# A new order of work in the two state-space mixers of a ten-stage kernel

## The chip, the cores and the metric

One Trainium2 chip, one core of it. The time is device microseconds from the start of the program to its end. The kernel runs on five engines that follow their own instruction queues and meet at semaphores: PE (matrix products into the eight PSUM banks), DVE (vector), ACT (scalar functions from tables), POOL (a second vector engine) and SP, whose queue here only issues DMA transfers. Every array of the calculation is float32.

## The reference, cut to what matters

`x` has two rows (sequences) of 512 tokens and 256 features. Four layers follow one another, each as half a feed-forward block, a mixer, half a feed-forward block. The change lies in the mixers of layers 2 and 3 and in the feed-forward block ahead of layer 2's mixer:

```python
x = x + 0.5 * _L2_ffn_ref(_layernorm(x), ...)     # top 1 of 8 dense experts
x = x + _L2_attn_ref(_layernorm(x), ...)          # mixer, 8 heads of 64
x = x + 0.5 * _L2_ffn_ref(_layernorm(x), ...)
x = x + 0.5 * _L3_ffn_ref(_layernorm(x), ...)     # top 2 of 8 gated experts and a shared one
x = x + _L3_attn_ref(_layernorm(x), ...)          # mixer, 64 heads of 64
x = x + 0.5 * _L3_ffn_ref(_layernorm(x), ...)
```

Both mixers compute the same thing, in layer 3 with eight times as many heads:

```python
zxbcdt = u @ W_in                     # z, x|B|C and one dt for each head
dt = softplus(dt + dt_bias)
xBC = silu(conv4(xBC) + conv_b)       # 4 taps along the tokens
A = -exp(A_log)                       # decay of a token: exp(A * dt)
Y_diag = einsum('bcln,bcsn,bhcls,bcshp->bclhp', Cm, Bm, Lmat, x * dt)
states = einsum('bcln,bhcl,bclhp->bchpn', Bm, decay_states, x * dt)
Y_off  = einsum('bcln,bchpn,bhcl->bclhp', Cm, states_so_far, out_decay)
y = Y_diag + Y_off + x * D_param
yf = y * silu(z)
out = (yf * rsqrt(mean(yf * yf) + 1e-5) * norm_w) @ W_out
```

Within a chunk of tokens every token takes from the earlier ones, weighed by `Lmat` (`Y_diag`); between chunks a state of 128 by 64 for each head is carried on (`Y_off`).

## The kernel before, in words

**Tiles and steps.** `mamba` (L2079) serves both mixers. It cuts the tokens of a row into CB=4 chunks of 128. A unit is one row and one group of 8 heads, that is 512 inner columns in NM=4 pieces `m` of 128; a step is one chunk of one unit. Layer 2 has 2 units and 8 steps (`few` is true), layer 3 has 16 units and 64 steps. What is needed before the first step is the head (L2487 to L2575); the loop over the steps is L2589 to L2643.

**What sets the order.** The program's own order is written by hand. Inside `with self.in_order(tail)` (L230) each instruction of an engine is tied behind the one written before it on the same engine: in the head for PE, ACT and DVE, in the steps for POOL too. So each engine is a queue in the order of the calls, and an instruction that waits holds up all behind it on its engine. DMAs go out on SP's queue in the order written.

**The head.** `row(0)` makes the normalized, turned input `xT`; layer 2's comes already turned from the feed-forward block before (`next_measure` and `next_turn`, L1908 to L1920, into `nxT`). `decay_sums` (L2122) is a generator of which `next(d0)` runs one part: PE's product `pd` for `dt`, the softplus on ACT (`Exp`, then `Ln`), `dA`, row sums that go out to HBM as `rows` (L2171) and come back broadcast over all partitions, the sums `jb`, and last the exponentials `cd` (decay of a whole chunk) and `dec` (decay to a chunk's end), each a small PE product and an `Exp` (L2181). `conv` (L2188) is one convolution of 128 channels over a row: PE writes `pp`, ACT makes the first tap (L2196), DVE adds three taps (L2200), ACT does the SiLU (L2204). `conv_b` and `conv_c` do it for B and C; `prep_front` (L2273) for a piece of x, as `xc`, and `prep_back` (L2287) turns `xc` on PE, copies it on ACT as `xt` (L2291) and multiplies `xc` by D, for three pieces of the first unit on POOL (L2295), otherwise on ACT (L2297). `products` (L2217) are C times B of each chunk and `mask` (L2228) writes their lower triangle into the PSUM tile `M`, DVE into an SBUF tile `Msb` and ACT from there.

**The parts of a step `s`.** `chunk(s+3)` fetches the row sums by DMA into `lm` (L2308) and `ce` (L2311). `exponents` (L2316) are eight DVE operations on `lm`; `raised` (L2325) is ACT's `exp` of `lm` and `ce` together, 2048 columns, or `raised_alone` (L2328) of 1024; `masked` (L2331) is DVE's `lm` times `M`; `from_start` (L2337) is POOL's `ce` times C; `to_end` (L2358) is POOL's `xd`, x by `dec`. `z_gate` (L2343) is PE's product `pz` and ACT's SiLU of it, `sg`. `main` (L2366) is PE's `py` from `lm`, `xt`, `ce` and the state, and POOL's state by `cd` (L2385). `gate` (L2399) adds D's part on DVE and multiplies by `sg` on POOL; `squares` (L2405) and `all_squares` (L2418) sum y's squares, `project` (L2430) multiplies by `W_out` into `yacc`, `new_state` (L2387) makes `pst` on PE and adds it to the state. `add_row` (L2442) closes a row: the sum over channels `pr` (L2446), a root, and the add into `x` (L2451).

**The loop before**, the same for both layers: squares(s-1); chunk(s+3); at an odd chunk exponents(s+2), at an even one masked(s); the next unit's convolution and its taps; the turn of the piece before; z_gate(s+1); to_end(s); the SiLU of the new piece; raised(s+1) at an odd chunk, masked(s+1) at an even one; from_start(s+1); main(s); gate(s); at an even chunk exponents(s+2); all_squares and project(s-1); at the start of a row add_row of the row before; new_state(s). In layer 2's first two steps B's and C's convolution of the second row follow (`convs`). `prep_front` and `z_gate(0)` stand so that main(s) is written behind the convolution, the turn and the gate of the unit to come.

**Layer 3's expert rows.** The feed-forward block before leaves its experts' outputs in HBM. They are added to `x` by pending parts that `settle` (L261) runs: a DMA `y<-rows` (L857) and adds of 128x256 (L880), here on POOL. Row 1, the second one, is settled at the end of the head.

**PSUM.** In layer 2's feed-forward block one pool of eight banks, `psM`, serves the logits `pl`, the turned weights `ps_ct`, the experts' products `ps_y` and all turns.

## Time and profile before

| | us |
|---|---|
| median of 9 runs | 1840.26 |
| lowest and highest | 1836.88, 1846.09 |
| the profiled execution | 1833.76 |
| its span on the core | 1832.0 |
| layer 2's mixer in the trace, head and steps | 828 to 936 |
| layer 3's mixer, head | 1120 to about 1167 |
| layer 3's mixer, steps | to about 1720 |

The page of the profile gives each engine's busy time over the span, the same in 40 slices, the DMA queues, the chain of waits that ended last and the costliest groups of instructions. Three groups that belong to the mixers, each with its count, the busy time, the mean of one and the idle time just before it with what ended most of it:

```profile
L2200 DVE SCALAR_TENSOR_TENSOR xc<-pp,L_attn_cols,xc 128x511 f32<-128x511 f32 (+2 forms) x216 | 161.3, 748 | 25.3 <-ACT xc L2196 20.1
L2348 PE MATMUL pz<-lateT,wt 128*128 128x128 f32 x1024 | 125.8, 276 | 6.3 <-ACT xt L2291 4.1
L2433 PE MATMUL yacc<-wt,y 128*128 128x256 f32 x576 | 142.7, 391 | 0.6 <-DVE x L2451 0.3
```

Names come from the program: `xc<-pp` writes the tile `xc` from the tile `pp`. The line numbers are those of the kernel before. A view by windows gives the same busy times for stretches of the span, so that stages with different limits can be told apart, and a view in order of time gives start, length, engine, line and operation of each run of equal instructions, with the wait ahead of it in brackets.

### The profile page before, as it was taken

The page shows a single profiled execution, that of the slowest core. Times are in us where ns is not written, and L with a number is a line of the kernel's source. Part 1 is how long each engine was busy: PE and PEld are TensorE (multiplying, and loading weights), DVE is VectorE, ACT ScalarE, POOL GpSimd, SP SyncE. Part 2 cuts the span into 40 slices and gives each one's busy share as a digit, 9 for nine tenths or more (in the row PEclk, how much of TensorE's full clock was granted, in tenths as well). Part 3 has the DMA queues.
Part 4 walks back from the last instruction along what each step waited for, and adds up shares of the span by engine and source line. Part 5 has one row for each costly group of instructions (what it writes and reads, how often), then busy time and mean ns, then how long its engine had stood idle before and what let it go on. Part 6 is the DMA issues. An engine that isn't in the chain of part 4 may idle for free. (4 is left out here: it accounts for less than half of the span.)

```text
span 1832.0 us, 29511 instructions
## 1 busy us (share of the span) xinstructions
PE 1697.1 (93%) x10342; PEld 1220.7 (67%) x10342; DVE 1137.1 (62%) x2945; ACT 810.0 (44%) x1399; POOL 952.2 (52%) x974
## 2 busy tenths in 40 slices
PE   7999989999999889998889898799999999999994
PEld 4777756666777657545655476577777777777573
DVE  6433367346433479775867534887777887778633
ACT  1223235331223137315631123678877777777221
POOL 4777656514777441211440263546756656767373
PEclk9999999999999899999989999999999999999897
DMA  9466451142655510102300133444445444443133
GB/s 298 140 221 188 150 189 38 60 138 77 184 186 171 200 59 2 47 1 82 113 28 12 38 107 114 164 147 159 156 139 175 158 146 167 158 159 129 37 115 97
DMA packets 122197, 226.52 MB, mean 124 GB/s; under 512 B 22398, under 2 KB 74988, under 8 KB 121894
## 3 DMA queue, kind: packets, MB, share of 16 engines
q1 hardware_dynamic: 97046, 179.08, 29.5%
q0 software_dynamic: 18944, 42.16, 7.3%
q10 hardware_dynamic: 6032, 3.10, 0.6%
q8 instruction: 91, 1.49, 0.3%
q14 instruction: 84, 0.69, 0.1%
HBM read 195.59 MB, written 41.81 MB: 130 GB/s over the span
## 5 line engine op out<-in xcount | busy, mean ns | idle before, releaser
L645 POOL DMA_INDIRECT xe<-table,sl_get x176 | 183.0, 1040 | 145.1 <-DVE sl_get L617 88.1
L673 PE MATMUL ps_gu<-we,xeT 128*128 128x352 f32 x704 | 225.1, 460 | 0.0
L704 POOL DMA_INDIRECT rows<-ye,sl_put x176 | 177.1, 1006 | 88.3 <-issue 40.2
L2200 DVE SCALAR_TENSOR_TENSOR xc<-pp,L_attn_cols,xc 128x511 f32<-128x511 f32 (+2 forms) x216 | 161.3, 748 | 25.3 <-ACT xc L2196 20.1
L698 PE MATMUL ps_ye<-we,hT 88*128 88x256 f32 x704 | 168.2, 379 | 3.7 <-DVE hT L225 2.0
L678 DVE SCALAR_TENSOR_TENSOR he<-se,xe,ps_gu 128x176 f32<-128x176 f32 x176 | 69.9, 397 | 158.5 <-ACT se L677 150.5
L673 PEld LDWEIGHTS ps_gu<-we,xeT 128*128 128x128 f32 x704 | 126.1, 190 | 55.3 <-DVE xeT L225 1.4
L698 PEld LDWEIGHTS ps_ye<-we,hT 88*128 88x128 f32 x704 | 133.1, 190 | 37.9 <-ACT ye L227 3.6
L2321 DVE SCALAR_TENSOR_TENSOR lm<-lm,jb,top 128x128 f32<-128x128 f32 x576 | 153.5, 342 | 0.0
L2403 POOL TENSOR_TENSOR y<-y,sg 128x512 f32<-128x512 f32 x72 | 91.8, 1275 | 101.1 <-DVE y L2402 99.7
L2433 PE MATMUL yacc<-wt,y 128*128 128x256 f32 x576 | 142.7, 391 | 0.6 <-DVE x L2451 0.3
L677 ACT ACTIVATE se<-ps_gu 128x176 f32<-128x176 f32 x176 | 55.9, 318 | 183.8 <-PE ps_gu L673 183.8
L2348 PE MATMUL pz<-lateT,wt 128*128 128x128 f32 x1024 | 125.8, 276 | 6.3 <-ACT xt L2291 4.1
L2341 POOL TENSOR_TENSOR ce<-ce,CT 128x1024 f32<-128x1024 f32 x54 | 128.0, 2370 | 0.0
L2348 PEld LDWEIGHTS pz<-lateT,wt 128*128 128x128 f32 x1024 | 119.7, 192 | 9.5 <-ACT xt L2291 5.3
L1964 PE MATMUL ps_y<-w8T,xT 128*128 128x512 f32 x256 | 125.5, 620 | 0.0
L2193 PE MATMUL pp<-lateT,wx 128*128 128x512 f32 x256 | 121.8, 599 | 0.8 <-DVE xc L2200 0.8
L2433 PEld LDWEIGHTS yacc<-wt,y 128*128 128x128 f32 x576 | 103.8, 190 | 22.8 <-issue 9.3
L2414 POOL TENSOR_TENSOR sqs<-sqs,sq 128x512 f32<-128x512 f32 x56 | 71.3, 1274 | 85.4 <-ACT sq L2413 85.4
L2333 DVE TENSOR_TENSOR lm<-lm,M 128x1024 f32<-128x1024 f32 x72 | 87.2, 1215 | 39.3 <-ACT lm L2326 36.8
L2376 PE MATMUL py<-lm,xt 128*64 128x128 f32 x1152 | 107.1, 279 | 4.7 <-PE pz L2348 2.1
L2193 PEld LDWEIGHTS pp<-lateT,wx 128*128 128x128 f32 x256 | 48.6, 191 | 57.2 <-issue 52.3
(520 smaller groups left out, 3501.9 us busy)
## 6 DMA issues: line engine op xcount, KB each, us to landing
lm<-rows SPq DMA_DIRECT2D x72, 512.0 KB
ce<-rows SPq DMA_DIRECT2D x54, 512.0 KB
y<-rows SPq DMA_DIRECT2D x16, 768.0 KB
we<-in_L_ffn_w_gate_dram SPq DMA_DIRECT2D x64, 176.0 KB
we<-in_L_ffn_w_up_dram SPq DMA_DIRECT2D x64, 176.0 KB
we<-in_L_ffn_w_down_dram SPq DMA_DIRECT2D x64, 176.0 KB
we<-in_L_ffn_w_dram SPq DMA_DIRECT2D x48, 176.0 KB
wx<-in_L_attn_in_proj_w_dram SPq DMA_DIRECT2D x16, 512.0 KB
```

What stands on the lines that cost most here:

```text
L645: nc.gpsimd.indirect_dma_start(xe[:, i, :], None, table, bass.IndirectOffsetOnAxis(get[:, at + j : at + j + 1], 0), bounds_check=T - 1, oo ...
L673: nc.tensor.matmul(pg, xeT[:, k, i * P : (i + 1) * P], wgu[:, :, k], start=(k == 0), stop=(k == KD - 1))
L698: nc.tensor.matmul(py[:, i, :], hT[:, q, i * P : (i + 1) * P], wd[:, q, :], start=(q == 0), stop=(q == 1))
L704: put_rows = nc.gpsimd.indirect_dma_start(rows, bass.IndirectOffsetOnAxis(put[:, at + j : at + j + 1], 0), y[:, i, :], None, bounds_check= ...
L1964: nc.tensor.matmul(ps, xT[:, k, :], self.w8T[:, k, 2 * e2 : 2 * e2 + 2, :], start=(k == 0), stop=(k == KD - 1))
L2193: nc.tensor.matmul(pp, wv[:, k, :], xT[:, k, b * S : (b + 1) * S], start=(k == 0), stop=(k == KD - 1))
L2200: nc.vector.scalar_tensor_tensor(out[:, 3 - w :], pp[:, : S - 3 + w], cw[:, m, w : w + 1], out[:, 3 - w :], ALU.mult, ALU.add)
L2321: nc.vector.scalar_tensor_tensor(k["lm"][:, h, :], k["lm"][:, h, :], jb[:, k["c"], n : n + 1], top, ALU.add, ALU.min)
L2341: nc.gpsimd.tensor_tensor(k["ce"], k["ce"], ct, ALU.mult)
L2348: nc.tensor.matmul(pz[:, m, :], u["wz"][:, kk, m * P : (m + 1) * P], xT[:, kk, c * P : (c + 1) * P], start=(kk == 0), stop=(kk == KD - 1),)
L2376: nc.tensor.matmul(py[i * HP : (i + 1) * HP, m, :], w[:, h * HP : (h + 1) * HP], v[:, h, :], start=(m == 0 and n == 0), stop=(n == len(src ...
L2433: nc.tensor.matmul(yacc[cc // 2][:, cc % 2, :], k["y"][:, m, :], u["wo"][:, m, :], start=(u["g"] == 0 and m == 0 and cc % 2 == 0), stop=(u ...
```

## The change

**The feed-forward block ahead of layer 2's mixer** (`l2_ffn`). The logits and the turned weights get a PSUM pool of their own, `psG` with two banks (tags `pl` and `ct`), the rest keeps six. The last of the eight chunks is no longer normalized and turned for the mixer within the block: its scale is computed at the block's end, and the mixer calls `self.last()`, which centres it, and turns it in `decay_sums`, behind the first seven chunks of `pd`.

**Both mixers.** `cd` and `dec` share one tile and one `Exp`, so `decay_sums` has one part fewer. The first row's products are written into `M` itself and masked there. All four products of `xc` and D of the first unit are on POOL. `z_gate(0)` leaves the head and is issued in step 0; `masked(0)` enters the head, behind exponents(1).

**Layer 2.** The head has another order. The sum of squares over the four pieces is two adds on POOL in place of a reduction on DVE. The steps are issued by a function of their own, `short_step`, in which main(s), gate(s) and new_state(s) come ahead of the next convolution, turn, gate and the exponents and mask of the steps to come.

**Layer 3.** `settle(1)`, the DMAs and POOL's adds for the second row, moves from the end of the head to before `conv_c`; C's taps come ahead of the chunks' DMAs, the products ahead of the first SiLU of x. The steps are as before, apart from `z_gate(0)` and `masked(0)`.

The core of the diff, with eight columns of indent taken off:

```diff
@@ -1863,6 +1863,7 @@
+    self.lastn = keep.tile([P, D], F32, name="lastn")
@@ -1892,7 +1893,8 @@
-    psM = es.enter_context(tc.tile_pool(name="f2m", bufs=8, space=PSUM))
+    psG = es.enter_context(tc.tile_pool(name="f2g", bufs=1, space=PSUM))
+    psM = es.enter_context(tc.tile_pool(name="f2m", bufs=6, space=PSUM))
@@ -2025,8 +2027,9 @@
-        next_measure(NC - 1)
-        next_turn(NC - 1)
+        if into is not None:
+            mv, rstd = self.scale(self.keep, "n_last", NC - 1)
+            self.last = lambda: self.centre(self.lastn, NC - 1, mv, rstd)
@@ -2112,8 +2115,8 @@
-    dec = sb.tile([P, NC, nh], F32, name="dec")
-    cd = sb.tile([P, NC, nh], F32, name="cd")
+    falls = sb.tile([P, 2, NC, nh], F32, name="falls")
+    cd, dec = falls[:, 0], falls[:, 1]
@@ -2126,9 +2129,11 @@
-        pd = psM.tile(sh, F32, tag="mm", name="pd")
+        pd = (psA if few else psM).tile(sh, F32, tag="py" if few else "mm", name="pd")
         for cc in range(nb * CB):
             c = b * CB + cc
+            if few and c == NC - 1:
+                turn_last()
@@ -2178,12 +2183,17 @@
-        for out, lhsT in ((cd, self.ones), (dec, self.c["gt"])):
-            ps = aux.tile(sh, F32, tag=tag, name="ps_dec")
-            nc.tensor.matmul(ps, lhsT, da, start=True, stop=True)
-            nc.scalar.activation(out[:, bs, :], ps, AF.Exp)
-            yield
+        ps = aux.tile([P, 2] + sh[1:], F32, tag=tag, name="ps_dec")
+        for i, lhsT in enumerate((self.ones, self.c["gt"])):
+            nc.tensor.matmul(ps[:, i], lhsT, da, start=True, stop=True)
+        nc.scalar.activation(falls[:, :, bs, :], ps, AF.Exp)
+        yield
         nc.vector.tensor_tensor(dec[:, bs, :], dec[:, bs, :], d, ALU.mult)
+
+    def turn_last():
+        for k in range(KD):
+            nc.tensor.transpose(M[:, k, :], self.lastn[:, k * P : (k + 1) * P], self.ident)
+        nc.scalar.copy(xT[:, :, T - P :], M[:, :KD, :])
@@ -2226,11 +2236,12 @@
-        m = wk.tile([P, CB, P], F32, tag="xd", name="Msb")
+        m = M if pm is M else wk.tile([P, CB, P], F32, tag="xd", name="Msb")
         nc.vector.tensor_tensor(
             m, pm, self.c["le"][:, :P].unsqueeze(1).to_broadcast([P, CB, P]), ALU.mult
         )
-        nc.scalar.copy(M, m)
+        if pm is not M:
+            nc.scalar.copy(M, m)
@@ -2291,7 +2302,7 @@
-        if u["b"] == u["g"] == 0 and m < NM - 1:
+        if u["b"] == u["g"] == 0:
             nc.gpsimd.tensor_scalar(u["xc"][:, m, :], u["xc"][:, m, :], dcol[:, n : n + 1], None, ALU.mult)
@@ -2421,9 +2432,14 @@
+            if few:
+                half = sqs[:, cc, : 2 * P]
+                nc.gpsimd.tensor_tensor(half, half, sqs[:, cc, 2 * P :], ALU.add)
+                nc.gpsimd.tensor_tensor(sqm[0][:, cc, :], half[:, :P], half[:, P:], ALU.add)
+            else:
+                nc.vector.tensor_reduce(
+                    sqm[0][:, cc, :], sqs[:, cc, :].rearrange("p (m t) -> p t m", m=NM), AX.X, ALU.add
+                )
@@ -2494,14 +2510,15 @@
         if few:
             b_taps, b_silu = conv_b(0)
             c_taps, c_silu = conv_c(0)
+            self.last()
+            unit(0)
             b_taps()
+            x = [prep_front(us[0], 0)]
             c_taps()
+            x[0][0]()
             next(d0)
-            unit(0)
...
             next(d0)
             b_taps()
             unit(0)
+            self.settle(1, adder=nc.gpsimd)
             c_taps, c_silu = conv_c(0)
             next(d0)
             x = [prep_front(us[0], 0), prep_front(us[0], 1)]
             next(d0)
+            c_taps()
@@ -2512,65 +2529,60 @@
-        if not few:
+        if few:
+            x.append(prep_front(us[0], 2))
+            b_silu()
+            c_silu()
+            fill(4)
+            pm = products(0)
+            x[0][1]()
+            x[2][0]()
+            next(d0)
+            x.append(prep_front(us[0], 3))
+            x[1][1]()
+        else:
...
-            c_taps()
...
+            pm = products(0)
...
+        mask(pm)
+        prep_back(us[0], 0)
+        if not few:
             x[2][0]()
-        else:
-            x.append(prep_front(us[0], 2))
-            b_silu()
-            c_silu()
-            x[0][1]()
-            fill(4)
-            x[2][0]()
-            next(d0)
-            x.append(prep_front(us[0], 3))
-            x[1][1]()
-        pm = products(0)
...
-        if few:
-            x[3][0]()
-            mask(pm)
-        else:
-            mask(pm)
-            x[3][0]()
+        x[3][0]()
         prep_back(us[0], 1)
         x[3][1]()
         prep_back(us[0], 2)
-        z_gate(ks[0])
...
         next(d0)
-        next(d0)
         exponents(ks[1])
+        masked(ks[0])
         raised_alone(ks[1])
         next(d0, None)
-        if few:
-            later = {}
-        else:
-            self.settle(1, adder=nc.gpsimd)
+        if not few:
             parts = [lambda: measure(1), None, lambda: norm(1), lambda: turn(1, 0), lambda: turn(1, 1)]
-            parts += [d1.__next__] * 8 + [lambda: next(d1, None)]
+            parts += [d1.__next__] * 7 + [lambda: next(d1, None)]
@@ -2585,8 +2597,69 @@
-    convs = ((0, 0), (0, 1)) if few else ((NG - 4, CB - 1), (NG - 3, CB - 1))
+    convs = (NG - 4, CB - 1), (NG - 3, CB - 1)
+    def short_step(s):
+        n, cc = steps[s]
+        nxt, row_end = n + 1 < len(order), cc == CB - 1
+        k, ahead = ks[s], s + 2 < NS
+        nonlocal back
+        with self.in_order(tail):
+            if s > 0:
+                squares(ks[s - 1])
+            chunk(s + 3)
+            if back and cc == 0:
+                prep_back(*back)
+                back = None
+            if cc == 0 and s > 0:
+                masked(k)
+            rest = None
+            if s == 0:
+                taps, rest = prep_front(unit(n + 1), cc)
+                z_gate(k)
+            to_end(k)
+            main(k)
+            gate(k)
+            if s + 1 < NS:
+                from_start(ks[s + 1])
+            if s > 0:
+                all_squares(ks[s - 1])
+            new_state(k)
+            if cc % 2 and ahead:
+                exponents(ks[s + 2])
+                raised(ks[s + 1])
+            if nxt:
+                if s > 0:
+                    taps, rest = prep_front(unit(n + 1), cc)
+                taps()
+            if back:
+                prep_back(*back)
+                back = None
+            if s + 1 < NS:
+                z_gate(ks[s + 1])
+            if rest:
+                rest()
+                back = (us[n + 1], cc)
+            if s > 0:
+                project(ks.pop(s - 1))
+            if (n, cc) == (0, 0):
+                both(conv_b(1))
+            elif (n, cc) == (0, 1):
+                both(conv_c(1))
+            if cc % 2 == 0:
+                if ahead:
+                    exponents(ks[s + 2])
+                masked(ks[s + 1])
+            elif not row_end:
+                masked(ks[s + 1])
+            if n and cc == 0:
+                add_row(n - 1)
+            if nxt and row_end:
+                mask(products(1))
...
     for s in range(NS):
+        if few:
+            short_step(s)
+            continue
@@ -2601,7 +2674,7 @@
-            elif cc % 2 == 0:
+            elif cc % 2 == 0 and s > 0:
@@ -2610,6 +2683,8 @@
+            if s == 0:
+                z_gate(k)
```

More of the change, by code (lines that the diff above doesn't have):

```diff
@@ L1939, in gates @@
                     return
-                pl = psM.tile([P, E], F32, tag="mm", name="pl")
+                pl = psG.tile([P, E], F32, tag="pl", name="pl")
                 for k in range(KD):
@@ L1973, in bias_turn @@
                     return
-                ct = psM.tile([E, P], F32, tag="mm", name="ps_ct")
+                ct = psG.tile([E, P], F32, tag="ct", name="ps_ct")
                 nc.tensor.transpose(ct, ws[c], self.ident)
@@ L2218, in products @@
                 pb = psM.tile([P, CB, P], F32, tag="mm", name="pb")
-                pm = psM.tile([P, CB, P], F32, tag="mm", name="pm")
+                pm = psM.tile([P, CB, P], F32, tag="mm", name="pm") if b else M
                 for cc in range(CB):
@@ L2423, in all_squares @@
                         sqm[0] = wk.tile([P, CB, P], F32, tag="cr", name="sqm", bufs=1)
-                    nc.vector.tensor_reduce(
-                        sqm[0][:, cc, :], sqs[:, cc, :].rearrange("p (m t) -> p t m", m=NM), AX.X, ALU.add
-                    )
+                    if few:
[6 more added lines that the diff above has]
+                        )
             yacc = [psA.tile([P, 2, D], F32, name=f"yacc{i}") for i in range(CB // 2)]
@@ L2496, in mamba @@
                     c_taps, c_silu = conv_c(0)
+                    self.last()
+                    unit(0)
                     b_taps()
+                    x = [prep_front(us[0], 0)]
                     c_taps()
+                    x[0][0]()
                     next(d0)
-                    unit(0)
-                    x = [prep_front(us[0], 0)]
+                    x.append(prep_front(us[0], 1))
                     next(d0)
-                    x[0][0]()
-                    x.append(prep_front(us[0], 1))
                     next(d0)
@@ L2535, in mamba @@
                     x[1][1]()
+                mask(pm)
+                prep_back(us[0], 0)
+                if not few:
                     x[2][0]()
-                else:
-                    x.append(prep_front(us[0], 2))
-                    b_silu()
-                    c_silu()
-                    x[0][1]()
-                    fill(4)
-                    x[2][0]()
-                    next(d0)
-                    x.append(prep_front(us[0], 3))
-                    x[1][1]()
-                pm = products(0)
-                prep_back(us[0], 0)
-                x[2][1]()
-                if few:
-                    x[3][0]()
-                    mask(pm)
-                else:
-                    mask(pm)
-                    x[3][0]()
+                x[2][1]()
+                x[3][0]()
                 prep_back(us[0], 1)
```

## The prediction

> **What bounds the kernel now.** I read the page first, then busy time by stage, then the order of time inside the two stages that the diff touches.

> ```profile
> span 1832.0 us, 29511 instructions
> PE 1697.1 (93%) x10342; PEld 1220.7 (67%) x10342; DVE 1137.1 (62%) x2945; ACT 810.0 (44%) x1399; POOL 952.2 (52%) x974
> ...
> PE 4%; issue 1%; DMA 1%; POOL 0%; DVE 0%; ACT 0%; SPq 0%; POOLq 0%; ACTq 0%
> ```

> PE is the bound as a mean. The chain of waits breaks off after some 6% of the span, so it says nothing of the mixers; the stages must be read by windows (columns: stretch, length, busy time and count of PE, PEld, DVE, ACT, POOL, then granted clock, DMA share, GB/s):

> ```profile
> 828.00:870.00 42.00, 33.55 (x163) 22.25 (x161) 25.21 (x57) 23.87 (x38) 8.81 (x7) 0.92 0.26 90
> 870.00:935.00 65.00, 59.18 (x458) 45.71 (x458) 50.74 (x98) 41.82 (x56) 30.85 (x22) 1.00 0.26 91
> ...
> 1120.00:1160.00 40.00, 34.55 (x152) 23.35 (x151) 28.89 (x65) 19.39 (x30) 11.86 (x15) 0.95 0.67 222
> 1160.00:1720.00 560.00, 540.99 (x4022) 417.21 (x4022) 435.44 (x922) 416.50 (x573) 359.58 (x275) 0.99 0.43 146
> ```

> Layer 2's mixer takes 828 to 936: a head, then 8 steps in 65.5 us, of which PE idles only 5.8. Layer 3's has the head from 1120 and 64 steps in which PE idles 3%. So in layer 2 a new order of steps can win 6 us at most and lose without limit, and in layer 3 what the head gains is kept, since PE carries it on. Step 1 of layer 2, in order of time:

> ```profile
> 879.49 2.31 DVE L2200 SCALAR_TENSOR_TENSOR xc<-pp,L_attn_cols,xc 128x511 f32<-128x511 f32 x3
> 882.64 1.28 ACT L2326 ACT_TABLE_LOAD   x1
> 883.94 1.91 ACT L2326 ACTIVATE lm<-lm 128x2048 f32<-128x2048 f32 x1
> 884.47 0.69 DVE L2395 TENSOR_TENSOR state<-state,pst 128x512 f32<-128x512 f32 x1 [1.10 <-PE pst L2391]
> 886.84 2.32 DVE L2200 SCALAR_TENSOR_TENSOR CT<-pp,L_attn_cols,CT 128x511 f32<-128x511 f32 x3 [1.68 <-ACT CT L2196]
> 889.07 1.21 DVE L2333 TENSOR_TENSOR lm<-lm,M 128x1024 f32<-128x1024 f32 x1
> ```

> The taps of the next unit (879.49) and the exponents run while PE does other work; the mask (889.07) is the last thing that the next `main` needs, and PE reaches that `main` at 891.25, just after a z gate. Layer 3's first step:

> ```profile
> 1166.25 3.03 POOL L880 TENSOR_TENSOR x<-x,y 128x256 f32<-128x256 f32 x4 [2.60 <-DMA y<-rows]
> ...
> 1169.24 1.04 POOL L2364 TENSOR_TENSOR xd<-xt,dec 128x512 f32<-128x512 f32 x1
> ...
> 1170.33 1.13 PE L2391 MATMUL pst<-xd,Bt 128*128 128x512 f32 x2 [1.96 <-POOL xd L2364]
> ```

> PE waits 1.96 for `xd`, which stands on POOL behind the expert rows.

> **Layer 2's head.** I lay the new order of each engine end to end, each instruction at its duration in this trace (taps 2.32, eight exponents 2.15, `exp` of 1024 columns 1.06, mask 1.21, table load 1.28, SiLU 0.72, conv 1.9 on PE and 0.69 on ACT, z gate 1.95). PE idles from 828.57 to 831.53 for the last chunk's layernorm and 832.43 is the first conv. Now that chunk is turned behind `pd`'s first seven chunks; the first conv waits for the last read of the FFN's PSUM, DVE's at 829.4, so it starts 2.95 earlier. Of that, 1.0 is left at the `Ln`, since ACT's product of the second conv now stands ahead of its table load (0.7+1.28), and 1.3 at the row sums and their DMA (DVE's taps of `xc0` now lie ahead of `dt`). Products come 1.5 earlier, but the fourth conv is now behind them on PE, so both exponents end at 863.4, not 861.97. The first gate no longer stands before ACT's first `exp` (862.5, was 863.45), the fourth `xc` product (0.73 ACT) is on POOL (1.56 there, hidden: `xd` needs POOL at 865, and it ends at 863), one `exp` for `cd` and `dec` (0.26, between the rows of 0.21 at 64 and 0.37 at 256 columns) replaces two, `masked(0)` follows at once. `M` in place saves ACT 0.57. Main(0) starts at 864.9, was 870.13: -5.3, of which 1.95 is only that one z gate is moved behind it.

> **Layer 2's steps.** What counts is what stands before `masked(s+1)` on DVE, for PE is now sent straight to `main(s+1)`, with no next conv, turn and gate in front (4.4 us of PE work that covered the wait).
> - Step 0: state copy and z(1) wait on PSUM that `sg(0)` frees at 867.5; z(1) 1.95, conv_b 1.9, ACT 0.7 (872.15), then on DVE B's taps 2.32, exponents(2) 2.15, mask 1.21: main(1) at 877.9. 13.05; before 9.48 (870.13 to 879.61).
> - Step 1: main 1.95, state by `cd` on POOL 1.05, state add 0.7, exponents(3) 2.15, ACT's `exp` of 2048 columns 1.95, conv product 0.7 (ACT's queue holds it behind that `exp`), turn 0.58, D product 0.73, table 1.28, gate 0.6, weight 0.5, SiLU 0.72, C's product 0.69, then C's taps 2.35 and the mask 1.2. With 0.2 of handovers 17.35; before 11.64.
> - Step 2: main 1.95, pst 1.05, conv 1.95, ACT 0.7, taps 2.35, exponents(4) 2.15, mask 1.2: 11.4; before 10.36.
> - Step 3: main 1.95, y 0.7, exponents(5) 2.15, `exp` 1.95, ACT 0.7, taps 2.35, products 1.3 (their PSUM waits for these taps), Msb 0.7, SiLU-copy-copy tail on ACT 1.25, mask 1.2: 14.3; before 9.02.
> - Step 4: PE-bound with POOL's new half sums (0.75 at 256 columns by the row adds, 3.01 for four; 0.4 at 128, between 0.22 for one column and that 0.75) before xd(5): 6.85; before 5.81. Step 5: add_row ahead of y, then exponents(7), `exp`, mask: 9.2; before 7.31. Step 6: 7.0; before 4.67. Step 7 to the last row sum: 6.5; before 7.23.

> Together 85.7 against 65.5: +20.2; with the head +14.9. The FFN behind waits for the last add of the row in both, so it moves by the same. DVE's reduce (1.05 a step) goes to POOL: no gain, as DVE is not late by its load but by its order. The FFN's bank split (two for logits, six for the rest) costs nothing: the nearest reuse is a half iteration, 4.8 us, and DVE's lag there is up to 3.3; 1 us if that cover were gone.

> **Layer 3.** Row 1's expert DMAs now go on SP ahead of the second unit's weights, 1 MB more before `rows` (1143.7): at the 222 GB/s of that stretch the queue is 5 MB since 1120, empty about then; up to 2 us late at the worst, against 7 of slack of `lm`. POOL adds them at 1134 to 1140, free before `xc` at 1152.6. DVE, laid end to end: C's taps 1140.7 to 1143.0, row sums' copy to 1143.7 (1.1 late), `jb` after PE's sums to 1145.5, two taps to 1150.1, mask in place to 1150.8, two taps to 1155.4, exponents to 1159.65 (was 1160.75). ACT has no gate and no M copy before its first `exp`: 1158.8, was 1161.77. PE has conv and both gates done by 1163.3, where main(0) starts (was 1167.28); `xd` is there at 1162.6, pst(0) runs at once; conv, turn (SiLU 1165.8) and z(2) to 1170, main(1) to 1171.9, project, pst, conv, turn to 1177.4, z(3) to 1179.4, and main(2) when mask(2) is done, 1180.5: was 1185.64, with the same PE work behind it. Carried on the same way main(4) is 3.7 early, as the taps then bind. I take -4.5, between -1 (only the 1.96 wait, half kept) and -8 (all of PE's 5.1 idle in 1160 to 1180, and the slow spell).

> **The clock.**

> ```profile
> 862.00:864.00 2.00, 0.00 (x0) 0.00 (x0) 0.00 (x0) 1.97 (x3) 0.00 (x0) 1.00 0.62 252
> 864.00:866.00 2.00, 1.33 (x3) 0.93 (x4) 0.35 (x2) 1.23 (x4) 0.00 (x0) 0.60 0.00 0
> 866.00:868.00 2.00, 2.00 (x4) 0.85 (x3) 1.01 (x1) 0.57 (x1) 1.97 (x2) 0.55 0.00 0
> ```

> After 3.66 us without a matmul (861.0 to 864.67) PE runs some 4 us at 0.55; one conv took 3.26 for 1.88. The new order makes two waits of about 6 us (before main(1) and main(2)). Each costs 0 (if the spell falls on `py`, at most 324 ns for 273) to 1.5; I take +1 for both, bounds 0 and +4.

> [...]

> **Sum.** +14.9 -4.5 +1 = +11.4. The profiled execution took 1833.76 (span 1832.0 and 1.76 around it), so 1845.2 there; it lies 6.5 below the median of the nine, so 1840.26+11.4 = 1851.7. Its own bounds: layer 2 +10 (10% of the steps' chains too long, -9, half allowed) to +19 (0.5 a step of handovers unseen), layer 3 -8 to -1, clock 0 to 4: +2 to +22, 1842 to 1862.

> **Rivals.**
> - *PE still bounds layer 2's steps.* For: DVE's and ACT's busy shares are 78% and 64% there. Then main(1) starts when conv_b ends, 871.4, and what follows is PE work alone, 58.2: end 929.6, -6, with layer 3 -10.5: 1829.8. Against: masked(1) is behind B's taps on DVE, and no queue is passed. It decides if main(1) starts before 874.
> - *Layer 3 gives nothing back* (rows late behind 1 MB more DMA, or its loop's own waits eat it): +15.9 and up: 1856. For: DMA share 0.67 in the head. Against: `lm`'s slack.
> - *The two cancel*: half of layer 2's new waits, all of layer 3's gain: 1840.

> **Chances.** Forecast 0.68, layer 3's gain lost 0.17, PE-bound 0.09, cancelling 0.06. The range 1842 to 1862 leaves out the PE-bound rival, most of the cancelling one and a tail. What a measurement tells from no change is 0.2%, 3.7 us: slower 0.85, within 0.06, faster 0.09.

> **What would show it.** In the new trace: first conv some 3 us earlier after the FFN; PE idle of 5 us or more before main(1) and main(2), released by DVE's `lm<-lm,M`; steps 1 and 3 of 17 and 14 us; a half clock after them; layer 3's pst(0) with no wait for `xd`. Wrong if the eight steps take under 72 us, or layer 3's loop starts no earlier.

## The result, and the profile after

| | before | after |
|---|---|---|
| median, us | 1842.6 (62 runs) | 1858.14 (20 runs) |
| ratio to before, 95% interval | | 1.0086 [1.0075, 1.0098] |
| the profiled execution, us | 1833.76 | 1860.45 |

The change makes the kernel slower, by 15.5 us; 11.4 was forecast. The windows of the kernel after, stretch for stretch those shown of the kernel before (stretch, length, busy time and count of PE, PEld, DVE, ACT, POOL, granted clock, DMA share, GB/s):

```profile
828.00:870.00 42.00, 35.53 (x147) 21.42 (x146) 25.90 (x59) 19.08 (x31) 7.19 (x7) 0.92 0.24 90
870.00:935.00 65.00, 47.09 (x291) 33.93 (x289) 34.58 (x71) 32.45 (x47) 22.55 (x21) 0.84 0.22 74
...
1120.00:1160.00 40.00, 34.58 (x155) 27.01 (x154) 15.81 (x39) 7.65 (x20) 17.55 (x23) 0.96 0.37 125
1160.00:1720.00 560.00, 543.03 (x3976) 414.97 (x3976) 443.86 (x934) 423.22 (x585) 352.66 (x266) 0.99 0.45 153
```

In the second row PE is busy 47.09 of 65 us where it was 59.18, at a clock of 0.84 where it was 1.00, and no other engine has taken its place: DVE, ACT and POOL are all less busy than before. Nothing is saturated; the engines wait for each other. Step 1 of layer 2 after, in order of time (the shift of the whole stage against before is 5.15 us, and arose ahead of the mixer):

```profile
883.25 1.22 DVE L2344 TENSOR_TENSOR lm<-lm,M 128x1024 f32<-128x1024 f32 x1
...
884.57 0.69 PE L2387 MATMUL py<-lm,xt 128*64 128x128 f32 x4 [6.37 <-issue]
...
888.18 2.08 PE L2402 MATMUL pst<-xd,Bt 128*128 128x512 f32 x2
...
890.36 0.69 DVE L2406 TENSOR_TENSOR state<-state,pst 128x512 f32<-128x512 f32 x1 [1.39 <-PE pst L2402]
...
890.96 2.15 DVE L2332 SCALAR_TENSOR_TENSOR lm<-lm,jb,top 128x128 f32<-128x128 f32 x8
...
893.15 1.91 ACT L2337 ACTIVATE lm<-lm 128x2048 f32<-128x2048 f32 x1 [9.24 <-DVE lm L2332]
...
895.67 2.32 DVE L2210 SCALAR_TENSOR_TENSOR xc<-pp,L_attn_cols,xc 128x511 f32<-128x511 f32 x3 [2.55 <-ACT xc L2206]
...
900.25 2.32 DVE L2210 SCALAR_TENSOR_TENSOR CT<-pp,L_attn_cols,CT 128x511 f32<-128x511 f32 x3 [2.27 <-ACT CT L2206]
902.48 1.21 DVE L2344 TENSOR_TENSOR lm<-lm,M 128x1024 f32<-128x1024 f32 x1
...
903.75 0.69 PE L2387 MATMUL py<-lm,xt 128*64 128x128 f32 x4 [5.61 <-DVE lm L2344]
```

Two readings. The mask at 902.48 is the last thing that main(2) needs, and it stands behind both sets of taps and their waits for ACT, as the prediction laid it out; for main(1) the view names no releaser (`issue`), but the mask ahead of it ends at 884.47, 0.1 us before main(1) starts. And main(1) to main(2) takes 19.18 where it laid out 17.35: `pst` takes 2.08 for 1.1. The clock says why (windows of 2 us of the same kernel, around the start of main(1)):

```profile
880.00:882.00 2.00, 0.00 (x0) 0.00 (x0) 1.96 (x6) 0.64 (x2) 0.00 (x0) 1.00 0.00 0
882.00:884.00 2.00, 0.00 (x0) 0.00 (x0) 2.00 (x7) 1.89 (x3) 0.00 (x0) 0.88 0.00 0
884.00:886.00 2.00, 1.43 (x14) 1.46 (x16) 0.47 (x1) 0.00 (x0) 0.00 (x0) 0.50 0.03 8
886.00:888.00 2.00, 2.00 (x22) 1.84 (x18) 0.00 (x0) 0.00 (x0) 0.00 (x0) 0.50 0.00 0
888.00:890.00 2.00, 2.00 (x5) 0.84 (x3) 0.69 (x1) 0.00 (x0) 1.61 (x2) 0.50 0.58 168
```

PE waits from 878.2 to 884.57, the clock falls near the wait's end, and the half clock (0.50) lies on all of main(1) and on `pst`, which the state, the exponents and the mask then wait for.

The stages are compared by lengths of their own. In layer 2 the head runs from the last bias product of the feed-forward block ahead to main(0), the steps from main(0) to the first turn of the block behind; in layer 3 the lengths are from its `pd` product to main(0) and to its last row sum. All fourteen profiles:

| kernel | layer 2: head | steps | both | layer 3: to main(0) | whole mixer |
|---|---|---|---|---|---|
| before | 44.56 | 70.98 | 115.54 | 35.37 | 577.3 |
| after | 41.41 | 97.09 | 138.50 | 35.67 | 575.5 |
| old_loop | 41.61 | 72.68 | 114.29 | 36.37 | 576.2 |
| short_only | 46.09 | 96.68 | 142.77 | 37.79 | 578.8 |
| mask_first | 43.92 | 81.02 | 124.94 | 35.70 | 575.6 |
| fill_waits | 41.63 | 94.96 | 136.59 | 34.53 | 574.4 |
| fill_half | 38.61 | 90.88 | 129.49 | 35.51 | 575.4 |
| l3_only | 43.77 | 70.53 | 114.30 | 35.15 | 575.0 |
| settle_late | 41.39 | 97.09 | 138.48 | 34.42 | 578.3 |
| settle_mid | 40.29 | 96.15 | 136.44 | 35.96 | 576.0 |
| settle_gated | 40.30 | 96.14 | 136.44 | 34.30 | 574.2 |
| ln_first | 41.15 | 72.65 | 113.80 | 33.66 | 573.7 |
| dve_reduce | 42.71 | 70.99 | 113.70 | 35.17 | 575.0 |
| combined | 41.14 | 70.97 | 112.11 | 34.29 | 574.2 |

The steps repeat to about 1 us between kernels that share them; the head of layer 2 does not (38.61 to 43.92 for one and the same head), so a single head tells nothing under some 5 us.

### The profile page after: what moved, and what is told of

Its sections match the earlier page's. It is cut to its first block, busy times and chain, and to the rows that moved or that the text cites. A ratio compares the mean times of both kernels' runs of the same rounds, so it can differ in the third digit from the quotient of the medians.

```text
span 1858.6 us, 29522 instructions
## 1 busy us (share of the span) xinstructions
PE 1711.8 (92%) x10342; PEld 1232.0 (66%) x10342; DVE 1130.6 (61%) x2937; ACT 801.9 (43%) x1389; POOL 964.4 (52%) x992
## 5 line engine op out<-in xcount | busy, mean ns | idle before, releaser
L2387 PE MATMUL py<-lm,xt 128*64 128x128 f32 x1152 | 111.6, 288 | 24.7 <-issue 12.6
L2387 PEld LDWEIGHTS py<-lm,xt 128*64 128x64 f32 x1152 | 70.5, 141 | 37.2 <-issue 15.4
```

What stands on the lines that cost most here:

```text
L2387: nc.tensor.matmul(py[i * HP : (i + 1) * HP, m, :], w[:, h * HP : (h + 1) * HP], v[:, h, :], start=(m == 0 and n == 0), stop=(n == len(src ...
```

## The experiments

The kernels ran on several chips. On some of them the program is slower as a whole, the kernel before at 1933 to 1938 us; most of it is lost ahead of layer 2's mixer, which begins at about 900 us there. Each ratio is against the kernel before on the same chip, and the lengths of stages are compared across chips.

**old_loop.** From the kernel after, the steps of layer 2 in the order before:

```diff
-            convs = (NG - 4, CB - 1), (NG - 3, CB - 1)
+            convs = ((0, 0), (0, 1)) if few else ((NG - 4, CB - 1), (NG - 3, CB - 1))
...
             for s in range(NS):
-                if few:
-                    short_step(s)
-                    continue
                 n, cc = steps[s]
```

> The changed kernel with layer 2's steps issued in the order of the kernel before (one loop for both layers again); heads, POOL's half sums and layer 3 stay changed. Measured so far: layer 2's steps, from main(0) to the first turn of the feed-forward block behind, went from 70.98 to 97.09 us, the head to main(0) was 3.15 shorter. Theory A (the order of the steps on DVE is the whole loss): steps back to 71 to 74 (z gate(0) now lies in step 0), so layer 2 is 0 to 3 under the kernel before, and the whole run 1 to 5 us under it. Theory B (the head's rearrangement, the bank split or the half sums on POOL carry part of the loss): steps stay above 80, whole run still over the kernel before by more than 5.

Measured: ratio 0.9965 [0.995, 0.9979], steps 72.68, layer 2's mixer 1.25 under the kernel before. Theory A holds: with its other parts kept, the change is faster than the kernel before. The order of layer 2's steps is the loss, but for the 1.7 us that the steps are still longer (see dve_reduce).

**short_only.** The kernel before with `short_step` alone (its gate of chunk 0 and first mask as before).

> The kernel before with nothing changed but the order of layer 2's steps, which is that of the changed kernel (gate of chunk 0 and the first mask as before). Theory A: steps 94 to 98 us instead of 70.98, whole run 20 to 26 us over the kernel before in the profile. Theory B: the loss comes from the combination with the new head, so steps under 85 and less than 14 over.

Measured: ratio 1.0139 [1.0112, 1.0166], that is +25.6 us; steps 96.68. Theory A again: the order costs the same without the new heads.

**mask_first.** From the kernel after:

```diff
+                    if cc % 2 == 0:
+                        masked(ks[s + 1])
                     new_state(k)
-                    if cc % 2 and ahead:
+                    if ahead:
                         exponents(ks[s + 2])
+                    if cc % 2 and ahead:
                         raised(ks[s + 1])
+                    if cc % 2 and not row_end:
+                        masked(ks[s + 1])
...
-                    if cc % 2 == 0:
-                        if ahead:
-                            exponents(ks[s + 2])
-                        masked(ks[s + 1])
-                    elif not row_end:
-                        masked(ks[s + 1])
```

> The changed kernel with exponents(s+2) and masked(s+1) written ahead of the next unit's taps and of B's and C's taps in each step of layer 2. PE still goes from one main to the next with the same work between. Theory A (what stands ahead of the mask on DVE sets the next main): main(0) to main(1) falls from 12.4 to 9 to 10, main(1) to main(2) from 19.2 to under 13, steps 78 to 86 in all, 10 to 18 us under the changed kernel. Theory B (the engine that sets the end is ACT with its table loads, or PE at a half clock): steps above 92.

Measured: ratio 1.0016 [1.0001, 1.0031] against the changed kernel's 1.0086, steps 81.02. main(0) to main(1) takes 5.59, even less than expected, and main(1) to main(2) 13.70, somewhat more. In order of time, from main(0) on:

```profile
880.34 1.21 DVE L2344 TENSOR_TENSOR lm<-lm,M 128x1024 f32<-128x1024 f32 x1
881.47 2.15 DVE L2332 SCALAR_TENSOR_TENSOR lm<-lm,jb,top 128x128 f32<-128x128 f32 x8
883.54 2.31 DVE L2210 SCALAR_TENSOR_TENSOR xc<-pp,L_attn_cols,xc 128x511 f32<-128x511 f32 x3
...
884.11 0.44 PE L2387 MATMUL py<-lm,xt 128*64 128x128 f32 x4
```

The mask is done at 881.55, 4.3 us before the taps, and PE reaches main(1) with hardly a wait. The same instructions in another place on one queue are worth 16.1 us of the 26.1 that the steps had lost, with the clock in it: of the five slow mains only main(6) is left. Of the 10 us that remain, 8.8 lie in steps 1, 3 and 5 (13.70, 13.83 and 9.26 for 11.64, 9.02 and 7.31), where the exponents and ACT's `exp` stand between one main and the next, 3.4 in step 6 with the slow main(6) and 1.4 in step 4, while step 0 is 3.9 shorter than before; that these are the causes was read, not tried.

**fill_waits and fill_half.** From the kernel after, products of no use ahead of some mains, into the bank that main writes next:

```diff
+                for _ in range({1: 10, 2: 9, 3: 3, 4: 3, 6: 4}.get(k["s"], 0) if few else 0):
+                    nc.tensor.matmul(py[:, :2, :], self.ident, self.c["le"][:, :D], start=True, stop=True)
```

This is fill_half; fill_waits had 20, 18, 6, 5 and 8.

> The changed kernel with matmuls of no use written into py's own bank on PE ahead of main(1), (2), (3), (4) and (6): 20, 18, 6, 5 and 8 of 128x256, 4.7, 4.3, 1.4, 1.2 and 1.9 us at 236 ns each, less than the wait there. The order and all waits stay. In the changed kernel py(1), py(2), py(3), py(4), py(6) took 3.6, 3.6, 2.55, 1.9, 3.5 us where 1.95, 1.95, 1.95, 1.1, 1.95 is usual. Theory C (the half clock after the waits is some 6 to 8 us of the loss, not the 1 of the prediction): these come back, steps 89 to 92 instead of 97.09. Rival (the slow products are hidden behind DVE's queue anyway, as the prediction had it): steps within 1.5 of 97.

Measured: ratio 1.0112 [1.0088, 1.0135], steps 94.96. The dose was wrong: a filler took 0.44 us, not 0.236, and the 20 ended 2.3 us after the mask. The clock stayed at 1.00 over main(1) and main(2), and even so the steps were 2 us shorter.

> As fill_waits, with half the fillers: each 128x256 product in float32 shows as two matmuls and takes 0.47 us, so the 20 and 18 of fill_waits ran 8.8 and 7.9 us, over the waits; now 10, 9, 3, 3 and 4 ahead of main(1), (2), (3), (4) and (6), 4.7, 4.2, 1.4, 1.4 and 1.9 us, less than the waits of 6.4, 5.6, 2.4, 1.9 and 2.7. Theory C (the half clock after the waits costs some 5 us): every py at full clock (1.97 with state, 1.09 without), main(1) to main(2) 16.5 to 17.5 instead of 19.2, steps from main(0) to the next feed-forward block 90.5 to 93 instead of 97.1. Rival (DVE's queue hides the slow products): 95.5 to 97.5.

Measured: ratio 1.0057 [1.0028, 1.0087], steps 90.88, 6.2 less than in the kernel after. Main(1) to main(2) took 17.95, a little over what was expected, for one spell was left, which the windows show from the end of the fillers on:

```profile
951.00:953.00 2.00, 2.00 (x10) 1.53 (x9) 1.96 (x7) 1.00 (x2) 0.00 (x0) 1.00 0.00 0
953.00:955.00 2.00, 0.14 (x1) 0.00 (x0) 2.00 (x5) 1.52 (x2) 0.00 (x0) 1.00 0.00 0
955.00:957.00 2.00, 1.85 (x30) 1.85 (x32) 0.09 (x1) 0.00 (x0) 0.00 (x0) 0.87 0.00 0
957.00:959.00 2.00, 2.00 (x8) 1.02 (x5) 0.69 (x1) 0.00 (x0) 1.26 (x2) 0.50 0.38 109
```

After 2.0 us without a product the clock fell again, for 3.4 us. So what the half clock costs is 6.2 us or more; against settle_mid and settle_late, which have the steps of the kernel after and ran on the chip of fill_half, it is 5.3 and 6.2. Theory C holds; the rival, which the prediction leaned on, falls.

**l3_only.** Layer 2 and its feed-forward block as before, layer 3's mixer as after.

> Layer 2 and the feed-forward block ahead of it as in the kernel before, layer 3's mixer as in the changed kernel. Layer 3's mixer, from its pd product to its last row sum, was 577.3 and 578.8 us in the two profiles that have the old layer 3 and 574.4 to 576.2 in the four that have the new one. Theory D (the new layer 3 gains some 2.5, less than the 4.5 predicted, as half of the head's gain is lost on DVE and on PE's clock): 575 to 576, whole run 1 to 4 us under the kernel before. Rival (the prediction's 4.5, hidden in the profiles by layer 2's shift): 573 to 574, whole run 4 to 6 under.

Measured: ratio 0.9982 [0.9955, 1.0008], the mixer 575.0. The ratio alone can't tell theory D from no change. The mixer's length fits D; the eight profiles that have this layer 3 unchanged lie at 573.7 to 576.2, 575.1 in the mean, against 578.05 for the two old ones: -2.9, and the rival's 573 to 574 is reached by one.

**settle_late.** From the kernel after:

```diff
-                    self.settle(1, adder=nc.gpsimd)
                     c_taps, c_silu = conv_c(0)
...
                 if not few:
+                    self.settle(1, adder=nc.gpsimd)
                     parts = [lambda: measure(1), None, lambda: norm(1), lambda: turn(1, 0), lambda: turn(1, 1)]
```

> The changed kernel with layer 3's settle of the second row where the kernel before has it, at the end of the head. By the prediction the early adds take away a wait of 1.96 us of PE for xd ahead of the first pst. Theory: without them that wait is back, 1.5 to 3.5 us, main(0) to main(1) of layer 3 takes 7.5 to 9.7 us instead of 6.0, and DVE's dt operations take 0.42; the mixer 576 to 578. Rival (the wait went away with the gate that left the head, not with the early adds): main(0) to main(1) stays at 6.0 to 6.5 and the mixer at 574 to 575.

Measured: ratio 1.0105 [1.0063, 1.0147], the mixer 578.3. The first `pst` of layer 3 in the kernel after, with no wait, and then in settle_late:

```profile
1196.45 1.12 PE L2402 MATMUL pst<-xd,Bt 128*128 128x512 f32 x2
```

```profile
1287.19 1.12 PE L2402 MATMUL pst<-xd,Bt 128*128 128x512 f32 x2 [1.60 <-POOL xd L2375]
```

The wait for `xd` is back, 1.60, main(0) to main(1) 7.69; the rival falls. The late rows then cost more further on: the statistics of the second row wait for them on DVE, with the exponents behind, and PE waits another 2.08 before main(2). Against the mean of 575.1 the early adds are worth 3 us: they are the part of layer 3's change that gains.

**settle_mid and settle_gated.** The adds behind DVE's operations on `dt`. settle_mid only writes `settle` further down (ahead of the second part of the head); settle_gated also makes each add wait for the last operation on `dt`:

```diff
+                    dt_last = self.last_on("DVE")
+                    n_traced = len(nc.cur_bb.bb.instructions)
+                    self.settle(1, adder=nc.gpsimd)
+                    for add in nc.cur_bb.bb.instructions[n_traced:]:
+                        if add.engine.name == "Pool":
+                            tc.add_manual_dep(add, dt_last.name, ...)
```

> The changed kernel with layer 3's settle of the second row written behind the row sums of the decays, ahead of the second part of the head, not ahead of C's convolution. Theory E (DVE's operations on two tensors, dt and dA, take 0.83 us beside POOL's row adds and 0.42 alone, and stand on the path to the row sums): with the adds moved behind them they take 0.42 each, the first main of layer 3 starts 34.3 to 34.7 us behind pd (35.4 to 36.4 in the profiles with the overlap), the mixer 574 to 575. Rival (the doubled time is hidden behind another wait): 35.4 or more, and if the row DMAs come late behind the chunks' and POOL's xd waits behind the adds, 37.

Measured: ratio 1.0109 [1.0065, 1.0154], main(0) at 35.96, the mixer 576.0. A miss that says nothing of theory E: POOL's order is not pinned in the head, so the adds started 3.6 us behind `pd`, no later than the 3.1 of the kernel after, and four of DVE's operations took 0.83 to 0.98.

> The changed kernel with layer 3's early row adds on POOL made to wait for DVE's last operation on dt (in settle_mid they had started as early as before, since nothing ordered them). Theory E (the adds hold DVE's two-tensor operations: dt and dA at 0.83 us beside them, 0.42 alone, on the path to the row sums): all four at 0.42 to 0.43, ps_row 0.9 to 1.5 earlier behind pd, main(0) 34.2 to 34.8 behind pd (35.96 in settle_mid, 35.67 in the changed kernel), the mixer 574 to 575. Rival (another wait ends last in the head): dt at 0.42 but main(0) at 35.4 or later.

Measured: ratio 1.0045 [1.0014, 1.0075], main(0) at 34.30, the mixer 574.2. First the kernel after, POOL's and DVE's rows, then settle_gated:

```profile
1162.89 6.36 POOL L880 TENSOR_TENSOR x<-x,y 128x256 f32<-128x256 f32 x8
1164.29 2.32 DVE L2210 SCALAR_TENSOR_TENSOR BT<-pp,L_attn_cols,BT 128x511 f32<-128x511 f32 x3 [0.44 <-ACT BT L2206]
...
1166.97 0.83 DVE L2152 TENSOR_TENSOR dt<-dt,dt 128x256 f32<-128x256 f32 x1
1167.84 0.83 DVE L2153 TENSOR_TENSOR dt<-dt,dA 128x256 f32<-128x256 f32 x1
1168.70 0.83 DVE L2154 SCALAR_TENSOR_TENSOR dA<-dt,nA 128x256 f32<-128x256 f32 x1
```

```profile
1243.37 0.42 DVE L2152 TENSOR_TENSOR dt<-dt,dt 128x256 f32<-128x256 f32 x1
1243.83 0.42 DVE L2153 TENSOR_TENSOR dt<-dt,dA 128x256 f32<-128x256 f32 x1
1244.28 0.42 DVE L2154 SCALAR_TENSOR_TENSOR dA<-dt,nA 128x256 f32<-128x256 f32 x1
...
1245.00 5.52 POOL L880 TENSOR_TENSOR x<-x,y 128x256 f32<-128x256 f32 x8 [7.03 <-DVE dt L2157]
```

Each of the three operations takes 0.83 beside POOL's adds and 0.42 alone. How many of them meet the adds differs from one profile to the next: in the four where none does (fill_waits by chance, settle_late, settle_gated, combined) main(0) lies at 34.29 to 34.53, in the others with the early adds at 35.15 to 36.37, but for ln_first, at 33.66 with one operation held. That the adds hold these operations is shown. That this sets main(0) is shown less well: with one of them held at 0.83, main(0) lies at 33.66 (ln_first), 35.17 (dve_reduce) and 36.37 (old_loop), so something else in this head moves it by up to 2.7 us, and what that is stays open.

**ln_first.** From old_loop, in layer 2's head:

```diff
                     next(d0)
+                    next(d0)
                     x.append(prep_front(us[0], 1))
-                    next(d0)
                     next(d0)
```

> old_loop with, in layer 2's head, the Ln of the softplus issued ahead of x's second convolution. In the changed kernel ACT's product of that convolution stands ahead of Ln's table load, waits for PE until 849.06, and DVE idles 4.79 us for dA; the prediction gave that 1.0. Theory F (this is the missing part of the head's gain): DVE's wait for dA falls under 2.2 us, the row sums leave 2.5 to 3.2 earlier, main(0) 38.2 to 39.7 us behind the last bias product (41.4 in the changed kernel, 41.6 in old_loop). Rival (the four x convolutions with their taps and table loads set the first exponents, the row sums have slack): main(0) at 40.8 or later, nothing gained.

Measured: ratio 0.9917 [0.9884, 0.9949], main(0) at 41.15: nothing gained that this noisy length could show, and the rival's outcome, though not its reason. DVE's wait for `dA`, in the kernel after and then here:

```profile
851.35 0.23 DVE L2151 SCALAR_TENSOR_TENSOR dt<-dt,dt 128x64 f32<-128x64 f32 x1 [4.79 <-ACT dA L2149]
```

```profile
912.54 0.23 DVE L2151 SCALAR_TENSOR_TENSOR dt<-dt,dt 128x64 f32<-128x64 f32 x1 [1.37 <-ACT dA L2149]
...
932.82 3.73 PE L2359 MATMUL pz<-nxT,wt 128*128 128x128 f32 x32
936.49 1.09 PE L2387 MATMUL py<-lm,xt 128*64 128x128 f32 x16
```

The wait did shrink by 3.4 us, and the first exponents came 1.6 us earlier behind the last bias product. But in the loop before, PE has both z gates in front of main(0), and they now end last, with no wait before main(0): PE's own work has taken the place of the wait.

**dve_reduce.** From old_loop, the sum of squares as one reduction on DVE again, the two adds on POOL removed.

> old_loop with layer 2's sum of squares as in the kernel before, one reduction on DVE a step instead of two adds on POOL. Theory G (the half sums stand on POOL ahead of what PE waits for at the row's change and cost the 1.7 us by which old_loop's steps are longer, 72.68 against 70.98 and 70.53): main(4) to main(5) falls from 7.43 to 5.8 to 6.2, steps 70.5 to 71.5. Rival (the gate moved into step 0 and the first mask are the cost): steps 72.2 to 73.

Measured: ratio 0.9932 [0.9904, 0.9961], steps 70.99, main(4) to main(5) 5.81. Theory G holds: in old_loop PE waits 1.34 in the row's sum `pr` for POOL's second half sum, with the next z gate behind it on its queue.

```profile
917.90 0.38 PE L2462 MATMUL pr<-cst,sqm 128*128 128x1 f32 x2 [1.34 <-POOL sqm L2438]
```

**combined.** The heads of the kernel after with the old steps, the reduction on DVE, `Ln` first and the gated adds.

> The changed heads of both layers with layer 2's steps in the order before, the sum of squares on DVE, Ln ahead of x's second convolution in layer 2's head, and POOL's row adds of layer 3 behind DVE's dt. If the parts add up: layer 2's mixer 113.0 to 114.0 us from the last bias product to the next feed-forward block (115.54 in the kernel before, 138.5 in the changed one), layer 3's 573.5 to 574.5 from pd to the last row sum (577.3, 575.5), together some 5 us under the kernel before and 26 under the changed one: ratio to the kernel before 0.995 to 0.998. If they don't: one of the two stages shows no gain over the single edits, and the ratio stays at 0.998 or above.

Measured: ratio 0.9941 [0.9917, 0.9966], faster than the kernel before. Layer 2's mixer is 112.11, 3.4 under before, layer 3's 574.2, 3.1 under it: the stages add up to 6.5 us, more than was expected of layer 2, whose head varies by some 5. The ratio says 11 us (6.6 to 16), more than the stages give and more than the 0.995 to 0.998 that were expected; where the rest comes from is not shown.

## Why the prediction was right, and where not

*What bounds.* Right. PE waits for DVE's mask before main(1) and main(2) as foretold; mask_first shows that the place of the mask on DVE makes 16 of the 26 us, old_loop and short_only that the order of the steps makes the loss. The rival that PE still bounds the steps is refuted: main(1) starts 12.4 us behind main(0), where it needed under 9.1.

*Layer 2's steps, +20.2.* Right in size, by cause. From main to main, laid out and measured: 13.05 and 12.44; 17.35 and 19.18; 11.4 and 12.83; 14.3 and 14.58; 6.85 and 8.03; 9.2 and 9.25; 7.0 and 8.07; 6.5 and 7.05 to the end of the last row sum. The sum is 85.7 against 91.4. What is missing is the clock: with most of the half clock removed (fill_half) the same eight are 12.39, 17.95, 11.07, 13.84, 7.25, 9.21, 6.47 and 7.07, none more than 0.7 from what was laid out and 85.3 together, and the steps to the next block are 19.9 above the kernel before.

*The clock, +1, bounds 0 to +4.* The term that was mis-sized. It counted two spells; the trace has five, over main(1), (2), (3), (4) and (6), of which the products took 3.68, 3.68, 2.71, 1.89 and 3.58 us for 1.97, 1.97, 1.97, 1.09 and 1.97, and fill_half measures 6.2 or more (5.3 against settle_mid). The bound above, +4, was too low as well. The reason given for the low value, that a spell falls on `py` at 324 ns for 273, fails: at half clock this `py` runs at 421 ns, and no `py` of the kernel before takes more than 324, so that figure was no measure of it. 6.2 over four or five spells is 1.2 to 1.6 each, where +1 for two counts 0.5.

*Layer 2's head, -5.3.* It measured -3.15 in the pair of profiles, and -3.7 between the means of three old heads (44.81) and of seven that are those of the kernel after (41.08). The start was right: the first conv comes 2.93 earlier behind the last bias product, 2.95 was forecast, and the split of the banks costs nothing that shows: the block ahead, from its first turn to its last bias product, takes 67.3 to 70.2 us with it and 69.0 to 70.2 without. The step that failed is the 1.0 "left at the `Ln`": DVE idled 4.79 us there, as the ACT product ahead of the table load waits for PE's second convolution. ln_first shows that wait shrink by 3.4 with `Ln` moved; how much of it main(0) of the kernel after would get back was not tried with the new steps.

*The half sums on POOL, "no gain".* They were a loss, 1.7 us with the old steps.

*Layer 3, -4.5.* The sign is right, the size about two thirds: -2.9 in the mean. The wait of 1.96 for `xd` is gone, as forecast, and comes back with the late adds. But the loop starts no earlier, which the prediction had named as a sign of being wrong: main(0) was laid out 31.4 us behind `pd` (1163.3 less 1131.91), and comes at 35.67, before at 35.37. The gain lies behind it. Main(0) to main(1) takes 6.02 for 9.74: 1.96 is the wait, and most of the rest is that PE's convolution and turn there no longer meet a half clock (1.88 and 0.60 us at a clock of 1.00, for 3.31 and 0.91 in the kernel before, with 0.50 from 1172 to 1174). Up to main(4) 1.7 of the 3.7 is lost again, 1.05 of it in a wait before main(2).

Two steps of the head failed. DVE's taps were laid end to end; but the third and fourth convolution of x now stand on PE behind the products, ran in part at a half clock (0.51 from 1177 to 1179), and DVE idles 2.08 for them (kernel after):

```profile
1177.46 5.09 PE L2203 MATMUL pp<-lateT,wx 128*128 128x512 f32 x8
...
1181.59 4.54 DVE L2210 SCALAR_TENSOR_TENSOR xc<-pp,L_attn_cols,xc 128x511 f32<-128x511 f32 x6 [2.08 <-ACT xc L2206]
```

And the early adds were taken as free: they end long before POOL is needed, but beside them three of DVE's operations on `dt`, ahead of the row sums, take twice their time (0.83 for 0.42). Together the exponents end 30.5 behind `pd`, where 27.7 was laid out. With the adds held back until those operations are done the mixer is 574.2 in both profiles, -3.9, near the forecast, though one profile without that gate reaches 573.7. How much the wait for the convolutions costs by itself was not tried. The rivals that layer 3 gives nothing back, or that the two parts cancel, are out by the mixer's length.

*The sum.* The range held, but that the forecast lies 4 us from the medians is in part luck. The medians give +15.5, 13.8 to 18.1 by the interval; the stages give +19.5 (steps +26.1, layer 2's heads -3.7, layer 3 -2.9), with all three on the slow side of what was forecast. By its number alone the rival in which layer 3 gives nothing back, +15.9, would have won. In the one pair of profiles the whole is +26.7, of which 5.15 arose ahead of the mixer. The whole run, by its ratio, lies between 2.5 us above and 10.7 below the sum of these stages (each against the one profile of the kernel before), furthest below in settle_gated, ln_first and dve_reduce (9.0 to 10.7); what makes this stays open, and a ratio by itself settles no difference of a few us here.

## What to carry to other kernels

An order that sends one engine straight to its next critical product is only as good as the queues of the engines that feed it: write the operation that it waits for ahead of all work for later on that queue, and keep work on the waiting engine to cover what remains. A wait on PE can cost twice, once as idle time and once in the clock of the very products that had been waited for: ahead of main(1) 6.37 us of waiting, and then 3.68 for 1.97 of products. And when a change has several parts, take them apart before giving it up: here one part lost over 20 us, a second 1.7, and the rest together was a gain.

## What was not expected of the hardware

Three of DVE's operations that read two SBUF tensors (L2152 to L2154) took 0.83 us each beside POOL's adds, also of two tensors, in the kernel after, and 0.42 alone in settle_gated; the one just ahead of them (L2151, two tensors as well) took 0.42 beside the adds in the kernel after and 0.98 in settle_mid. The eight adds took 6.36 together in the kernel after for 5.52 in settle_gated, while DVE's taps, which read PSUM and one SBUF tensor, kept their 2.32 beside them. An operation of one SBUF tensor can be held too: the maximum at L2145 took 0.28 us in settle_mid, where the adds start behind it, and 0.81 to 0.83 beside them in six profiles, as here in old_loop:

```profile
1138.83 0.81 DVE L2145 TENSOR_SCALAR dt<-dt 128x256 f32<-128x256 f32 x1
```

Both engines lose time in these rows; what makes them lose it, and whether the one waits for the whole of the other, the rows don't show.

```profile
931.16 1.89 PE L2387 MATMUL py<-lm,xt 128*64 128x128 f32 x16 [1.85 <-DVE lm L2344]
```

```profile
996.16 1.09 PE L2387 MATMUL py<-lm,xt 128*64 128x128 f32 x16 [1.84 <-DVE lm L2344]
```

Once begun, the five spells at 0.50 in the kernel after last 6.83, 6.83, 3.41, 3.41 and 3.41 us, and that of fill_half 3.41 (windows of 0.1 us added up).
